# Keys and values of a latent attention as pairs of half-height products on TensorE

## The chip, the cores and the metric

The kernel runs on one core of one Trainium2 chip, in float32. The metric is the device time of one execution in microseconds. TensorE multiplies; ScalarE, VectorE and GpSimd read and write the on-chip memory (SBUF), the first two also the accumulators (PSUM, eight banks of 128 partitions by 512 float32 columns); SyncE issues nearly all the transfers (DMAs), in one queue. Each engine executes its own instructions in the order in which they were written and waits on semaphores for the others.

## The reference, cut to what matters

The input is x of 8 batches, 512 tokens and 256 features. Four residual blocks follow each other: attention A, a feed-forward block (256 to 1024 to 256, relu), attention B (scores times a decay mask, no softmax), and the feed-forward block again with the same weights. Each is applied to a layer norm of x and added to x. The change lies in attention A, which has 16 heads of 16 features:

```python
q  = x @ Wq + bq
kv = (x @ Wkv_down + bkv_down) @ Wkv_up + bkv_up       # 256 -> 64 -> 512
k, v = jnp.split(kv.reshape(B, T, 16, 32), 2, axis=-1)
q, k = apply_rope(q), apply_rope(k)
att = softmax(q @ k.T / sqrt(16) + bias(distance))
out = att @ v
out = out + 0.2 * sigmoid(q @ mean_k) * mean_v
return out @ Wo + bo
```

The 64 features between Wkv_down and Wkv_up are the latent. Keys and values are products over these 64 features.

## The kernel before, in words

**Stages of one batch.** The front of attention A (`front1`, `front2`) makes from x the layer norm, its transpose `xT` (256 features in two chunks of 128 partitions, by 512 tokens), the latent `lat` (64 partitions by 512 tokens), then keys, queries and values, and the means for the last term. Scores and softmax run per group of four heads in steps. The rest (`rest`: output projection, feed-forward, attention B, feed-forward) runs in units on TensorE.

**Keys, queries, values.** `latent` (line 338) multiplies two chunks of `wd_sb` by `xT` into rows 0 to 63 of a bank, and ScalarE copies it out with the bias and a sum over tokens. `half_unit` (line 394) makes one rotary half (the first or second eight features of all 16 heads) of keys or queries: a product into one bank, for keys `wk_sb[:, e, :]` (64 rows by 128 columns) by the latent, and then two VectorE operations that multiply the biased result by the cosine and the sine table into `rc` and `rs` (names in the profile). `turn` adds and subtracts the halves on GpSimd, stores them to a DRAM buffer and loads them from there per head into `kT` or `qT`: two DMAs and four DMAs. `values` (line 347) makes the values of two of the four token tiles (128 tokens each): two products with a latent tile as the stationary operand into the two halves of one bank, then two VectorE additions of the bias row into `vaug`. It is called twice a batch.

**Operands' rows.** A product over 64 partitions uses the rows of TensorE at which its operands' partitions lie. All operands of the keys and values lie on partitions 0 to 63. The score products are over 32 partitions, one head each, at the four offsets 0, 32, 64 and 96; a step makes two score products for the row maxima (s in the profile), which go with two of the offsets, and two for the probabilities (t), which go with the other two.

**Banks.** Scores have two buffers of two banks, weighted values one bank, and everything else takes the next of a ring of three banks (`misc`, line 203). In the first 34 steps the t products take two banks of that ring as well. A bank is free for its next user when its readers have finished.

**The order of the work** is written out when the program is built. The front of batch 0 comes first, by hand: `order0[:8]` runs from the latent to the queries, then late loads, then `order0[8:12]`. From there a planner keeps a clock for each engine and a time at which each of the three banks comes free. Each `Unit` has a cost on TensorE in ns (`pe`), costs on other engines (`then`) and predecessors. Between steps the planner issues the unit that can start earliest, as a credit of TensorE time per step allows or when a unit fits in front of the next step (lines 745 to 790, and the loop at the end). So a changed cost can move other units.

The loads at the start stand in SyncE's queue in the order of the program (lines 108 to 129): x in two halves, `vec` (bias columns), `wd_sb`, `wk_in`, `wq_in`, the rotary tables, `wv_sb`, bias rows, and attention B's weights. `regroup` (line 209) sorts the columns of `wk_in` and `wq_in` by halves on ScalarE, ahead of the copies of the first `xT`.

Of the kernel before, what the change touches and what calls it, by code (L numbers as in the profile page):

```python
# [15 lines left out]
P = 128  # L16
B, T, D = 8, 512, 256
NH, HD = 16, 16
HH = 8
# [16 lines left out]
def tile_kernel(  # L36
# [74 lines left out]
    half = keep([P, NT], "half")  # L111
    gps.memset(half, -0.5)
    vec = resident(vecs, "vec")
    wd_sb = resident(wdown, "wd_sb")

    wk_in = at.tile([LAT, NH, 32], F32, tag="p", bufs=4, name="wk_in")
    move(wk_in.rearrange("p h d -> p (h d)"), wk[:, 0, :])
    wq_in = at.tile([P, NC, NH, 32], F32, tag="p", bufs=4, name="wq_in")
    move(wq_in.rearrange("p c h d -> p c (h d)"), wq[:, :, 0, :])

    rope_sb = keep([P, 2, T], "rope_sb")
    move(rope_sb, rope[0:HH].unsqueeze(0).to_broadcast([NH, HH, 2, T]))
    wv_sb = resident(wv, "wv_sb")
    row = keep([P, 2, D], "row")
    move(row[:, 0, :], rows[0:D].partition_broadcast(P))
    move(row[:, 1, :], rows[2 * D : 3 * D].partition_broadcast(P))
    wqk_in = rs.tile([P, NC, 2, D], F32, tag="big", bufs=1, name="wqk_in")
    move(wqk_in, wb[:, :, 0:2, :])
    bv, b2 = row[:, 0, :], row[:, 1, :]


    qT = [keep([P, NG, T], f"qT{i}") for i in range(2)]
# [72 lines left out]


    wq_sb = keep([P, NC, 2, P], "wq_sb")
    wk_sb = keep([LAT, 2, P], "wk_sb")
    def regroup():
        for e in range(2):  # L210
            half_of = slice(e * HH, (e + 1) * HH)
            act.copy(wk_sb[:, e, :].rearrange("p (h d) -> p h d", d=HH), wk_in[:, :, half_of])
        for e in range(2):
            half_of = slice(e * HH, (e + 1) * HH)
            for c in range(NC):
                act.copy(wq_sb[:, c, e, :].rearrange("p (h d) -> p h d", d=HH), wq_in[:, c, :, half_of])
# [64 lines left out]
    class Unit:  # L281
        def __init__(self, fn, pe=0, then=(), after=(), step=0, gives=None, needs=(), bank=True):
            self.fn, self.pe, self.then, self.after, self.step = fn, pe, then, list(after), step
            self.gives, self.needs, self.bank, self.done = gives, needs, bank and pe > 0, None
            self.takes = self.frees = False


# [49 lines left out]
    def front1(b):  # L337
        def latent():
            ps = misc(f"lat_{b}")
            for c in range(NC):  # L340
                mm(ps[:LAT, :], wd_sb[:, c, :], xT_a[b]["xT"][:, c, :], c == 0, c == NC - 1)
            lt = fr.tile([LAT, T], F32, tag="lat", name=f"lat_{b}")
            lsum[b] = fr.tile([LAT, 1], F32, tag="lsum", name=f"lsum_{b}")
            act.activation(lt, ps[:LAT, :], AF.Identity, bias=vec[:LAT, V_BD : V_BD + 1], accum_out=lsum[b])
            lat_a[b] = lt

        def values(h):
            ps = misc(f"v_{b}_{h}")
            for i in range(2):
                t = 2 * h + i  # L350
                mm(ps[:, i * D : (i + 1) * D], lat_a[b][:, t * P : (t + 1) * P], wv_sb)
            for i in range(2):
                dve.tensor_tensor(
                    vaug[b % 2][:, 2 * h + i, : NH * 17].rearrange("p (h d) -> p h d", d=17)[:, :, :HD],
                    ps[:, i * D : (i + 1) * D].rearrange("p (h d) -> p h d", d=HD),
                    bv.rearrange("p (h d) -> p h d", d=HD),
                    ALU.add,
                )


        def mean_v():
            ps = misc(f"mv_{b}")
            for c in range(NC):
                mm(ps[:, c : c + 1], wv_sb[:, c * P : (c + 1) * P], lsum[b])
            m = fr.tile([P, NC], F32, tag="mv_a", name=f"mv_a_{b}")
            dve.scalar_tensor_tensor(m, ps[:, :NC], 0.1 / T, bvc, ALU.mult, ALU.add)
            for c in range(NC):
                gps.tensor_scalar(vmean[:, c, : NH + 1], vmask[:, c, :], m[:, c : c + 1], None, ALU.mult)

        def through_wo():  # L370
            ps = misc(f"me_{b}")
            for c in range(NC):
                mm(ps[:, :D], vmean[:, c, :], wo_sb[:, c, :], c == 0, c == NC - 1)
            dve.tensor_add(mem[b % 2][: NH + 1, :], ps[: NH + 1, :D], bo_row[: NH + 1, :])

        s, (h0, h1) = ln_units(lambda: xs[b], f"a{b}", fr)
        free = PER * (b - 1) + LAG + PVLAG + 2
        u = {"lat": Unit(latent, 1720, (("ACT", 700),), after=[h0[2], h1[2]])}
        for h in range(2):
            u["v", h] = Unit(  # L380
                lambda h=h: values(h), 900, (("DVE", 850),), after=[u["lat"]], step=free
            )
        u["mv"] = Unit(mean_v, 250, (("DVE", 150), ("POOL", 400)), after=[u["lat"]])
        u["me"] = Unit(through_wo, 900, (("DVE", 400),), after=[u["mv"]], needs=(("wo", b - 2),))
        xT_a[b] = s
        return h0 + h1, u
# [3 lines left out]
    def front2(b, u1):  # L390
        rot = {}
        cos, nsin = rope_sb[:, 0, :], rope_sb[:, 1, :]

        def half_unit(j, e):
            ps = misc(f"{'qk'[j]}{e}_{b}")
            if j == 0:
                for c in range(NC):
                    mm(ps, wq_sb[:, c, e, :], xT_a[b]["xT"][:, c, :], c == 0, c == NC - 1)
            else:
                mm(ps, wk_sb[:, e, :], lat_a[b])  # L400
            for n, table in (("c", cos), ("s", nsin)):
                t = fr.tile([P, T], F32, tag="rot", bufs=6, name=f"r{n}{j}{e}_{b}")
                dve.scalar_tensor_tensor(t, ps, qk_bias[:, j, e : e + 1], table, ALU.add, ALU.mult)
                rot[n, e] = t

        def turn(j):

            d = (dq, dk)[j][b % 2]
            for e in range(2):
                o = rot["c", e]  # L410
                if e == 0:
                    gps.tensor_add(o, o, rot["s", 1])
                else:
                    gps.tensor_sub(o, o, rot["s", 0])
                move(d[:, e * HH : (e + 1) * HH, :], o)
            src = d.rearrange("(g s) r t -> s r g t", s=4)
            to = (qT, kT)[j][b % 2]
            for h in range(4):
                move(to[h * 32 : h * 32 + HD], src[h])
            if j == 0:  # L420
                if b > 1:
                    move(to[HD:P:32], zero_rows)
                rot["q"] = rot["c", 0], rot["c", 1]

        def mean_k():
            m = fr.tile([P, 2], F32, tag="mk", name=f"mk_{b}")
            for e in range(2):
                unused = fr.tile([P, T], F32, tag="unused", name=f"unused{e}_{b}")
                act.activation(unused, rot["c", e], AF.Identity, accum_out=m[:, e : e + 1])
                gps.tensor_scalar(kmean[:, e, :NH], hmask, m[:, e : e + 1], None, ALU.mult)  # L430

        def gate():
            ps = misc(f"ga_{b}")
            for e in range(2):
                mm(ps, kmean[:, e, :], rot["q"][e], e == 0, e == 1)
            act.activation(gates[b % 2][:NH, :], ps[:NH, :], AF.Tanh)

        free = PER * (b - 1) + LAG + PVLAG + 2
        lat = u1["lat"]
        rope = (("DVE", 1550),)  # L440
        k = [Unit(lambda e=e: half_unit(1, e), 950, rope, after=[lat]) for e in range(2)]
        kt = Unit(lambda: turn(1), then=(("POOL", 2600),), after=k, step=free)
        km = Unit(mean_k, then=(("ACT", 1200), ("POOL", 400)), after=[kt])
        q = [Unit(lambda e=e: half_unit(0, e), 1720, rope, after=[lat]) for e in range(2)]
        qt = Unit(lambda: turn(0), then=(("POOL", 2600),), after=q, gives=("qk", b))
        ga = Unit(gate, 1720, (("ACT", 600),), after=[km, qt], needs=(("wo", b - 2),))
        return [lat] + k + [kt, km] + q + [qt, u1["v", 0], u1["v", 1], ga, u1["mv"], u1["me"]]


    def score_item(n):  # L450
# [271 lines left out]
    n0[1].fn(), n1[1].fn()  # L722
    n0[2].fn(), n1[2].fn()
    memory_buffers()
    for u in order0[:8]:
        u.fn()
    late_loads()
    plain(0), plain(1)
    for u in order0[8:12]:
        u.fn()  # L730
    product(), product_biases()
    buffers(1, gps)
# [12 lines left out]
    def start_of(u):  # L745
        if any(x not in given for x in u.needs) or any(a.done is None for a in u.after):
            return None
        if u.takes and held:
            return None
        t = max([a.done for a in u.after] + [clock["PE"] if u.pe else 0])  # L750
        return max(t, banks[0]) if u.bank else t

    def fetch(b):
        xs[b] = load_x(b)
# [2 lines left out]
    def issue(u):  # L757
# [5 lines left out]
        for e, ns in u.then:  # L763
            clock[e] = t = max(clock[e], t) + ns + 60
        u.done = t
        if u.bank:
            banks.popleft()
            banks.append(t)
        if u.takes:
# [89 lines left out]

    posts = []  # L860
    setup = [Unit(lambda: fetch(2), step=20)]
    for u in front[0][0] + order0[:12]:
        u.done = 0
    order0[12].step = 10
    chains = [order0[12:], setup]
    for b in range(1, B):
        ln0, u1 = front1(b)
        ln0[0].step = ln0[3].step = max(0, PER * (b - 1) + 2)
# [165 lines left out]
```

## Time and profile before

| | |
|---|---|
| time of three runs, median (lowest to highest) | 1354.7 us (1354.05 to 1356.53) |
| the profiled execution's own time | 1355.33 us |
| its span, first to last instruction | 1353.5 us |
| TensorE products busy | 1278.4 us |
| VectorE busy | 805.8 us |
| ScalarE busy | 450.8 us |
| GpSimd busy | 408.3 us |
| mean granted TensorE clock | 0.977 |

PE is TensorE's products and PEld its weight loads, DVE is VectorE, ACT ScalarE, POOL GpSimd, SP SyncE. A group in the profile has the form output <- inputs, then rows and columns of TensorE, shapes and count; its columns are busy time, mean ns of one, and the idle time ahead of it with what ended most of it. Busy times of products overlap and their ends are modelled, so the start of the next operation is the better measure of what one costs. L198 is the helper that issues every product and L69 the one that issues the operations of the other engines, so the names of tiles tell the lines apart. A line of the list of waits has the total, the number of times and the longest, in us; a line of the timeline has start, length, what it is, and in brackets the idle time before it and what ended it.

### The profile page before, as it was taken

To read this page: it belongs to the slowest core of one execution; us is meant where nothing else is said; L and a number is where in the kernel's file an instruction comes from. 1 tells how busy PE (TensorE), PEld (TensorE's weight loads), DVE (VectorE), ACT (ScalarE), POOL (GpSimd) and SP (SyncE) were. 2 spreads that over 40 slices of the span, in tenths; PEclk is the share of its full clock that TensorE was granted. 3 is DMA by queue.
4 is the path that set the end of the run, shared out by engine and by line. 5 is a ranking of instruction groups with operands and counts; after the bars stand their busy time and mean duration, and the time that the engine had idled before them with its cause. 6 is when DMAs were issued, how large, how long until landed. Compare 5 with 4: busy or idle time off the path is not lost. (4 is left out here: it accounts for less than half of the span.)

```text
span 1353.5 us, 15551 instructions
## 1 busy us (share of the span) xinstructions
PE 1278.4 (94%) x6116; PEld 632.2 (47%) x6116; DVE 805.8 (60%) x1323; ACT 450.8 (33%) x646; POOL 408.3 (30%) x461
## 2 busy tenths in 40 slices
PE   7889998999899998999999999999999999999989
PEld 3323233535354553545544454535444554455665
DVE  4577976678656686546765667646755484433120
ACT  2034434342434324333343323342343233331201
POOL 4165443233422323223331414213321232222010
PEclk9689989999999999999999999999999999999999
DMA  4440040003000210004000300003000000000000
GB/s 122 134 79 1 1 79 1 1 16 64 1 1 1 63 33 1 0 5 91 1 1 1 68 28 1 1 1 79 1 1 0 17 1 1 1 16 1 0 16 16
DMA packets 22159, 32.09 MB, mean 24 GB/s; under 512 B 2987, under 2 KB 12652, under 8 KB 21806
## 3 DMA queue, kind: packets, MB, share of 16 engines
q1 hardware_dynamic: 21446, 30.83, 10.2%
q8 instruction: 48, 0.79, 0.3%
q10 hardware_dynamic: 640, 0.26, 0.1%
q14 instruction: 25, 0.20, 0.0%
HBM read 18.24 MB, written 12.58 MB: 23 GB/s over the span
## 5 line engine op out<-in xcount | busy, mean ns | idle before, releaser
L69 DVE TENSOR_REDUCE mr<-s 128x2 f32<-128x1024 f32 x256 | 312.4, 1221 | 274.9 <-PE t L198 264.5
L69 ACT ACTIVATE p<-t 128x1024 f32<-128x1024 f32 (+1 forms) x290 | 264.0, 924 | 554.4 <-PE t L198 496.1
L69 POOL TENSOR_TENSOR p<-p,dec_a 128x512 f32<-128x512 f32 x182 | 233.1, 1302 | 490.0 <-ACT p L69 435.6
L198 PE MATMUL s<-kT,qT 32*128 32x512 f32 x1024 | 297.6, 664 | 40.3 <-DVE mr L69 36.5
L198 PE MATMUL t<-qT,kT 32*128 32x512 f32 x1024 | 297.0, 647 | 4.8 <-DVE mr L69 2.5
L69 DVE TENSOR_TENSOR p<-p,dec_a 128x512 f32<-128x512 f32 x330 | 230.1, 738 | 21.5 <-ACT p L69 21.3
L198 PE MATMUL x<-w_sb,h_x 128*128 128x256 f32 x1024 | 233.1, 383 | 0.0
L198 PEld LDWEIGHTS x<-w_sb,h_x 128*128 128x128 f32 x1024 | 190.7, 190 | 52.5 <-issue 27.6
L198 PEld LDWEIGHTS s<-kT,qT 32*128 32x128 f32 x1024 | 81.1, 189 | 208.1 <-DVE mr L69 85.2
L198 PE MATMUL pv<-p,va 128*32 128x512 f32 x1024 | 152.2, 614 | 3.7 <-DVE p L69 3.1
L69 ACT ACTIVATE h_x<-hx,vec 128x512 f32<-128x512 f32 x128 | 88.0, 688 | 156.3 <-PE hx L198 156.3
L198 PE MATMUL hx<-xT_g,w_sb 128*128 128x512 f32 x256 | 122.1, 622 | 0.7 <-ACT xT_g L69 0.7
L198 PE MATMUL hx<-xT_f,w_sb 128*128 128x512 f32 x256 | 119.0, 604 | 0.0
L69 DVE TENSOR_TENSOR x<-x,x 128x256 f32<-128x256 f32 x64 | 27.1, 424 | 153.9 <-PE x L198 153.8
L198 PEld LDWEIGHTS t<-qT,kT 32*128 32x128 f32 x1024 | 80.4, 184 | 22.0 <-issue 9.1
L198 PEld LDWEIGHTS hx<-xT_g,w_sb 128*128 128x128 f32 x256 | 48.0, 196 | 67.7 <-issue 59.8
L198 PEld LDWEIGHTS hx<-xT_f,w_sb 128*128 128x128 f32 x256 | 46.2, 192 | 57.5 <-issue 54.3
L198 PEld LDWEIGHTS pv<-p,va 128*32 128x32 f32 x1024 | 23.6, 108 | 78.2 <-issue 35.4
L69 POOL TENSOR_TENSOR x<-x,row 128x256 f32<-128x256 f32 x64 | 47.7, 765 | 38.4 <-DVE xn_g L69 20.4
L69 POOL TENSOR_TENSOR rc<-rc,rs 128x512 f32<-128x512 f32 x32 | 42.6, 1354 | 10.9 <-DVE rs L69 10.9
L198 PE MATMUL bs<-xT_r,ret 128*128 128x512 f32 (+3 forms) x128 | 38.3, 442 | 0.4 <-DVE mv_a L69 0.4
L198 PE MATMUL bo<-ret 128*128 128x256 f32 x160 | 36.7, 382 | 0.0
(130 smaller groups left out, 1034.5 us busy)
## 6 DMA issues: line engine op xcount, KB each, us to landing
dk<-rc SPq DMA_DIRECT2D x16, 256.0 KB
kT<-dk SPq DMA_DIRECT2D x32, 128.0 KB
dq<-rc SPq DMA_DIRECT2D x16, 256.0 KB
qT<-dq SPq DMA_DIRECT2D x32, 128.0 KB
out_dram<-x SPq DMA_DIRECT2D x32, 128.0 KB
x<-in_x_dram SPq DMA_DIRECT2D x7, 512.0 KB
w_sb<-in_w_dram SPq DMA_DIRECT2D x2, 1024.0 KB
x<-in_x_dram SPq DMA_DIRECT2D x2, 256.0 KB
```

The source lines that it names most:

```text
L69: ins = f(*a, **k)
L198: tc.keep_in_program_order(nc.tensor.matmul(o, lhsT=l, rhs=r, start=start, stop=stop))
```

## The change

The latent is computed on both halves of the partitions: the down weights stand twice side by side in `wd_sb`, so that the same two products fill 128 rows of the bank, and the copy out and its sum run over 128 partitions. For this the down bias of `vec` is loaded also to partitions 64 to 127. `wv_sb` is loaded twice, to both halves of the partitions, and `wk_in` too; `wk_sb` has the first rotary half on partitions 0 to 63 and the second on 64 to 127.

The two products of the keys thereby use different halves of TensorE's rows and go into two banks, issued one after the other in one unit. Values of token tiles 0 and 2 use the lower half, of 1 and 3 the upper, with one bank for each half: four products in alternation, and then four additions. Keys and values are each one unit instead of two, with a cost on TensorE of 950 ns each instead of two of 950 and two of 900. Such a unit takes two of the ring's three banks, and the planner starts it when the second comes free. Four DMAs are added at the start.

```diff
-    wd_sb = resident(wdown, "wd_sb")
-
-    wk_in = at.tile([LAT, NH, 32], F32, tag="p", bufs=4, name="wk_in")
-    move(wk_in.rearrange("p h d -> p (h d)"), wk[:, 0, :])
+
+    wd_sb = keep([P, NC, 2, LAT], "wd_sb")
+    for j in range(2):
+        move(wd_sb[:, :, j, :], wdown)
+
+    wk_in = at.tile([P, NH, 32], F32, tag="p", bufs=4, name="wk_in")
+    for j in range(2):
+        move(wk_in[j * LAT : (j + 1) * LAT].rearrange("p h d -> p (h d)"), wk[:, 0, :])
...
-    wv_sb = resident(wv, "wv_sb")
+    wv_sb = keep([P, D], "wv_sb")
+    for j in range(2):
+        move(wv_sb[j * LAT : (j + 1) * LAT], wv)
...
     bv, b2 = row[:, 0, :], row[:, 1, :]
+    move(vec[LAT:, V_BD : V_BD + 1], vecs[:LAT, V_BD : V_BD + 1])
...
-    wk_sb = keep([LAT, 2, P], "wk_sb")
+    wk_sb = keep([P, P], "wk_sb")
     def regroup():
         for e in range(2):
             half_of = slice(e * HH, (e + 1) * HH)
-            act.copy(wk_sb[:, e, :].rearrange("p (h d) -> p h d", d=HH), wk_in[:, :, half_of])
+            act.copy(
+                wk_sb[e * LAT : (e + 1) * LAT, :].rearrange("p (h d) -> p h d", d=HH),
+                wk_in[e * LAT : (e + 1) * LAT, :, half_of],
+            )
...
-            self.gives, self.needs, self.bank, self.done = gives, needs, bank and pe > 0, None
+            self.gives, self.needs, self.banks, self.done = gives, needs, int(bank) if pe > 0 else 0, None
...
-                mm(ps[:LAT, :], wd_sb[:, c, :], xT_a[b]["xT"][:, c, :], c == 0, c == NC - 1)
-            lt = fr.tile([LAT, T], F32, tag="lat", name=f"lat_{b}")
-            lsum[b] = fr.tile([LAT, 1], F32, tag="lsum", name=f"lsum_{b}")
-            act.activation(lt, ps[:LAT, :], AF.Identity, bias=vec[:LAT, V_BD : V_BD + 1], accum_out=lsum[b])
+                mm(ps, wd_sb[:, c].rearrange("p j n -> p (j n)"), xT_a[b]["xT"][:, c, :], c == 0, c == NC - 1)
+            lt = fr.tile([P, T], F32, tag="lat", name=f"lat_{b}")
+            lsum[b] = fr.tile([P, 1], F32, tag="lsum", name=f"lsum_{b}")
+            act.activation(lt, ps, AF.Identity, bias=vec[:, V_BD : V_BD + 1], accum_out=lsum[b])
             lat_a[b] = lt
 
-        def values(h):
-            ps = misc(f"v_{b}_{h}")
+
+        def values():
+            ps = [misc(f"v_{b}_{j}") for j in range(2)]
             for i in range(2):
-                t = 2 * h + i
-                mm(ps[:, i * D : (i + 1) * D], lat_a[b][:, t * P : (t + 1) * P], wv_sb)
-            for i in range(2):
-                dve.tensor_tensor(
-                    vaug[b % 2][:, 2 * h + i, : NH * 17].rearrange("p (h d) -> p h d", d=17)[:, :, :HD],
...
+                for j in range(2):
+                    rows_of = slice(j * LAT, (j + 1) * LAT)
+                    t = 2 * i + j
+                    mm(ps[j][:, i * D : (i + 1) * D], lat_a[b][rows_of, t * P : (t + 1) * P], wv_sb[rows_of])
+            for j in range(2):
+                for i in range(2):
+                    dve.tensor_tensor(
+                        vaug[b % 2][:, 2 * i + j, : NH * 17].rearrange("p (h d) -> p h d", d=17)[:, :, :HD],
...
-        for h in range(2):
-            u["v", h] = Unit(
-                lambda h=h: values(h), 900, (("DVE", 850),), after=[u["lat"]], step=free
-            )
+        u["v"] = Unit(values, 950, (("DVE", 1650),), after=[u["lat"]], step=free, bank=2)
...
-        def half_unit(j, e):
+        def projected(j, e):
             ps = misc(f"{'qk'[j]}{e}_{b}")
...
-                mm(ps, wk_sb[:, e, :], lat_a[b])
+                rows_of = slice(e * LAT, (e + 1) * LAT)
+                mm(ps, wk_sb[rows_of], lat_a[b][rows_of])
+            return ps
+
+        def keys():
+            ps = [projected(1, e) for e in range(2)]
+            for e in range(2):
+                half_unit(1, e, ps[e])
+
+        def half_unit(j, e, ps):
...
-        k = [Unit(lambda e=e: half_unit(1, e), 950, rope, after=[lat]) for e in range(2)]
+        k = [Unit(keys, 950, rope + rope, after=[lat], bank=2)]
...
-        return max(t, banks[0]) if u.bank else t
+        return max(t, banks[u.banks - 1]) if u.banks else t
...
-        if u.bank:
+        for _ in range(u.banks):
             banks.popleft()
             banks.append(t)
```

The means of the values read the lower half of `wv_sb` and of the sums alone, and the counts of `order0` that are written out by hand follow the two units fewer (`[:7]`, `[7:10]`, `[10:]`).

More of the change, by code (lines that the diff above doesn't have):

```diff
@@ L340, in latent @@
             for c in range(NC):
-                mm(ps[:LAT, :], wd_sb[:, c, :], xT_a[b]["xT"][:, c, :], c == 0, c == NC - 1)
-            lt = fr.tile([LAT, T], F32, tag="lat", name=f"lat_{b}")
-            lsum[b] = fr.tile([LAT, 1], F32, tag="lsum", name=f"lsum_{b}")
-            act.activation(lt, ps[:LAT, :], AF.Identity, bias=vec[:LAT, V_BD : V_BD + 1], accum_out=lsum[b])
+                mm(ps, wd_sb[:, c].rearrange("p j n -> p (j n)"), xT_a[b]["xT"][:, c, :], c == 0, c == NC - 1)
+            lt = fr.tile([P, T], F32, tag="lat", name=f"lat_{b}")
+            lsum[b] = fr.tile([P, 1], F32, tag="lsum", name=f"lsum_{b}")
+            act.activation(lt, ps, AF.Identity, bias=vec[:, V_BD : V_BD + 1], accum_out=lsum[b])
             lat_a[b] = lt
-        def values(h):
-            ps = misc(f"v_{b}_{h}")
+        def values():
+            ps = [misc(f"v_{b}_{j}") for j in range(2)]
             for i in range(2):
-                t = 2 * h + i
-                mm(ps[:, i * D : (i + 1) * D], lat_a[b][:, t * P : (t + 1) * P], wv_sb)
-            for i in range(2):
-                dve.tensor_tensor(
-                    vaug[b % 2][:, 2 * h + i, : NH * 17].rearrange("p (h d) -> p h d", d=17)[:, :, :HD],
-                    ps[:, i * D : (i + 1) * D].rearrange("p (h d) -> p h d", d=HD),
-                    bv.rearrange("p (h d) -> p h d", d=HD),
-                    ALU.add,
-                )
+                for j in range(2):
[6 more added lines that the diff above has]
+                        vaug[b % 2][:, 2 * i + j, : NH * 17].rearrange("p (h d) -> p h d", d=17)[:, :, :HD],
+                        ps[j][:, i * D : (i + 1) * D].rearrange("p (h d) -> p h d", d=HD),
+                        bv.rearrange("p (h d) -> p h d", d=HD),
+                        ALU.add,
+                    )
         def mean_v():
@@ L363, in mean_v @@
             for c in range(NC):
-                mm(ps[:, c : c + 1], wv_sb[:, c * P : (c + 1) * P], lsum[b])
+                mm(ps[:, c : c + 1], wv_sb[:LAT, c * P : (c + 1) * P], lsum[b][:LAT])
             m = fr.tile([P, NC], F32, tag="mv_a", name=f"mv_a_{b}")
@@ L378, in front1 @@
         u = {"lat": Unit(latent, 1720, (("ACT", 700),), after=[h0[2], h1[2]])}
-        for h in range(2):
-            u["v", h] = Unit(
-                lambda h=h: values(h), 900, (("DVE", 850),), after=[u["lat"]], step=free
-            )
+        u["v"] = Unit(values, 950, (("DVE", 1650),), after=[u["lat"]], step=free, bank=2)
         u["mv"] = Unit(mean_v, 250, (("DVE", 150), ("POOL", 400)), after=[u["lat"]])
@@ L440, in front2 @@
         rope = (("DVE", 1550),)
-        k = [Unit(lambda e=e: half_unit(1, e), 950, rope, after=[lat]) for e in range(2)]
+        k = [Unit(keys, 950, rope + rope, after=[lat], bank=2)]
         kt = Unit(lambda: turn(1), then=(("POOL", 2600),), after=k, step=free)
         km = Unit(mean_k, then=(("ACT", 1200), ("POOL", 400)), after=[kt])
-        q = [Unit(lambda e=e: half_unit(0, e), 1720, rope, after=[lat]) for e in range(2)]
+        q = [Unit(lambda e=e: half_unit(0, e, projected(0, e)), 1720, rope, after=[lat]) for e in range(2)]
         qt = Unit(lambda: turn(0), then=(("POOL", 2600),), after=q, gives=("qk", b))
         ga = Unit(gate, 1720, (("ACT", 600),), after=[km, qt], needs=(("wo", b - 2),))
-        return [lat] + k + [kt, km] + q + [qt, u1["v", 0], u1["v", 1], ga, u1["mv"], u1["me"]]
+        return [lat] + k + [kt, km] + q + [qt, u1["v"], ga, u1["mv"], u1["me"]]
     def score_item(n):
@@ L724, in tile_kernel @@
     memory_buffers()
-    for u in order0[:8]:
+    for u in order0[:7]:
         u.fn()
@@ L728, in tile_kernel @@
     plain(0), plain(1)
-    for u in order0[8:12]:
+    for u in order0[7:10]:
         u.fn()
@@ L861, in tile_kernel @@
     setup = [Unit(lambda: fetch(2), step=20)]
-    for u in front[0][0] + order0[:12]:
+    for u in front[0][0] + order0[:10]:
         u.done = 0
-    order0[12].step = 10
-    chains = [order0[12:], setup]
+    order0[10].step = 10
+    chains = [order0[10:], setup]
     for b in range(1, B):
```

## The prediction

> **What bounds the kernel now.** I read first the page's busy table and its 40 slices:
>
> ```profile
> PE 1278.4 (94%) x6116; PEld 632.2 (47%) x6116; DVE 805.8 (60%) x1323; ACT 450.8 (33%) x646; POOL 408.3 (30%) x461
> PE   7889998999899998999999999999999999999989
> DVE  4577976678656686546765667646755484433120
> ```
>
> TensorE (PE) is the bound from about 290 us on: between 290 and 1200 us the table of windows gives it 880.45 of 910 us. Before that VectorE is close behind: 88.77 of 118.7 us between 39.3 and 158 us, with TensorE at a mean clock of 0.86. A microsecond taken from TensorE is worth a microsecond only where TensorE does not wait next. So the second view is the groups, with the changed operations (count, busy us, mean ns):
>
> ```profile
> L198 PE MATMUL k<-lat,wk_sb 64*128 64x512 f32 x32 | 17.6, 675 | 0.9 <-ACT lat L69 0.9
> L198 PE MATMUL lat<-xT_a,wd_sb 128*64 128x512 f32 x32 | 17.2, 663 | 1.4 <-ACT xT_a L69 1.4
> L198 PE MATMUL v<-wv_sb,lat 64*128 64x256 f32 x64 | 16.5, 392 | 0.2 <-ACT wr L69 0.2
> ```
>
> A float32 product is two passes, so 32 rows of k are two products in each of 8 batches. The third view is the list of waits. One entry matters, TensorE waiting for the row maxima that free a score bank:
>
> ```profile
> PE s L198 <- DVE mr L69: 36.5, 41, 1.9
> ```
>
> The fourth is the timeline, for what a pair costs. First a lone pair of 32-row score products (start, length), then the keys of batch 3:
>
> ```profile
> 280.95 1.13 PE L198 MATMUL t<-qT,kT 32*128 32x512 f32 x4 [0.15 <-DVE mr L69]
> 282.01 0.66 PE L201 MATMUL tr_a<-ident,xn_a 128*128 128x128 f32 x4
> ...
> 288.06 1.98 PE L198 MATMUL k<-lat,wk_sb 64*128 64x512 f32 x4
> 289.97 1.98 PE L198 MATMUL b<-xT_r,ct 128*128 128x512 f32 x4
> ```
>
> Four passes in two row groups take 282.01 - 280.95 = 1.06 us from start to next start; the same four passes of the keys, all on rows 0 to 63, take 1.91. And what follows the keys of batch 4:
>
> ```profile
> 422.35 1.98 PE L198 MATMUL k<-lat,wk_sb 64*128 64x512 f32 x4
> ...
> 424.80 0.74 DVE L69 SCALAR_TENSOR_TENSOR rc<-k,qk_bias,rope_sb 128x512 f32<-128x512 f32 x1
> ...
> 426.78 0.74 DVE L69 SCALAR_TENSOR_TENSOR rs<-k,qk_bias,rope_sb 128x512 f32<-128x512 f32 x1
> 426.78 1.13 PE L198 MATMUL s<-kT,qT 32*128 32x512 f32 x4 [0.17 <-ACT p L69]
> 427.44 1.21 DVE L69 TENSOR_REDUCE mr<-s 128x2 f32<-128x1024 f32 x1
> ...
> 428.70 1.13 PE L198 MATMUL t<-qT,kT 32*128 32x512 f32 x4 [0.79 <-DVE mr L69]
> ```
>
> The keys have ended at 424.26, but VectorE, full since 422.46, runs four rope operations to 427.44 and only then the maximum for which TensorE waits.
>
> **What the Trainium skill says.** TensorEngine Tiling (Array Packing), Available Configurations, lists 2x row tiling of 64x128 with two independent tiles. The trace shows the overlap for 32 rows (1.06 us above); nothing in it shows two 64-row tiles together. The same page's Gotcha 1 says that row tiles must not write one PSUM bank at a time; the change takes two banks. TensorE: Matmul & The Clock Gate, The mechanism, says weight loads overlap running products only where the row group differs, and LDWEIGHTS prices a load by columns, P/1.2 ns: the trace agrees, 146 ns mean for lat's 64 columns against 190 to 202 for 128.
>
> **The change, part by part.**
>
> *Keys.* Two products one after the other become a pair: 1.91 to 1.06, -0.85 us a batch. If 64-row tiles do not run together: 0. More than halving (-0.95) is excluded.
>
> *Values.* Eight passes of 256 columns take 1.92 us (308.73 to 310.65), a pass starting each 0.216 us in the run at 27.9 us. Now four rounds of two. A lone pair's round costs 0.53 for a pass that takes 0.43, so 0.10 us of weight load lies open. If that is open once: 4 x 0.22 + 0.10 = 0.97 us; if in each round: 4 x (0.22 + 0.10) = 1.28. No row shows successive rounds on one row group, so I take 1.1: -0.8, between -0.65 and -0.95 (0 without overlap).
>
> *Latent.* The same four passes, 64 columns more per load: 0.05 us, one load open, +0.05; up to 0.2 if all four are. ScalarE's copy costs the same on twice the partitions (682 ns is by its 512 columns; 128-partition copies of that length take 688).
>
> Sum: -0.85 - 0.8 + 0.05 = -1.6 us of TensorE time a batch, 7 x 1.6 = 11.2 us in the seven batches whose front is planned among other work.
>
> *VectorE* has the same operations, and ends them no earlier: after a pair, four ropes run from 1.06 to 1.06 + 4 x 0.66 = 3.7 us; before, the second half was ready at 1.91 and ended at about 1.91 + 1.4 = 3.3 to 3.8. Where TensorE next waits for VectorE the gain is swallowed. Going by the timeline with the order as it is:
> - keys of batches 2, 4, 6, 7: waits of 1.72, 0.17+0.79, 0.23+0.78, 0.17+0.80 us on ScalarE or the maxima follow within 8 us: 0. Batch 1: VectorE-bound, then 0.60 for a probability tile: 0. Batch 3: a 0.53 wait follows at 301.95: 0.3 left. Batch 5: 12 passes of hidden layer follow: 0.85.
> - values of batch 1: 2.31 us for a bank held by `va`: 0; batch 6: 1.40 on a maximum: 0; batch 2: 0.4, a step soon waits; batches 3, 4, 5, 7: 0.8 each.
>
> That is 0.3 + 0.85 + 0.4 + 3.2 = 4.75 us. But the order is not kept: the planner counts 950 ns where it counted 1900 (keys) and 1800 (values), sees VectorE's 3.1 us after the keys, and fills a gap ahead of a step with any unit that fits. Of the other 11.2 - 4.75 = 6.4 us I give it a little over a quarter: 6.5 us in all.
>
> *Banks.* Keys and values now take two of the ring's three banks at once. In all seven loop batches the keys already ran back to back, in five the values too, so the holding is much as before; I cost it at nothing, covered by the third bank. Without cover it is a wait like the 2.31 us.
>
> *Loads.* Four DMAs more on SyncE's queue: second wdown, wk, wv and 64 words of vec, by the issue rows 0.43 + 0.57 + 0.60 + 0.46 = 2.1 us. Two stand ahead of wq_in: 1.0 us, and 192 KB more at some 250 GB/s is 0.8. wq_in's copies began on ScalarE at 8.16, and the first latent-input copy queues behind them (9.02 to 9.61); the one that matters starts at 11.68 after transposes. 2.07 us of slack hides 1.0. The vec words are read at 16.03 and would be issued at about 8.5; the like-sized bvc took from 10.45 to 13.22. Hidden, unless it takes over 7 us. The gate, bo_row and bvc loads move back 2 us; GpSimd idles 8.70 us after them.
>
> *Start.* At the half clock a pair takes 2.0 us (the first 28 score passes, seven pairs, took 53.29 - 39.31 = 13.98). Keys start at 16.86, ropes at 19.0 as now, and end at 21.7 instead of 22.1; queries start 1.6 us earlier, but their DRAM stores stand behind the four kT loads on SyncE (27.68 to 29.43). First scores, now at 39.31, come 0.4 to 0.9 earlier: -0.5.
>
> Total -7.0 us. The profiled execution took 1355.33 us (span 1353.5, 1.8 around it), 0.6 above the median of 1354.7; 1355.33 - 7.0 = 1348.3 there, 1347.7 on the median's scale.
>
> **Rivals.**
> - *All of it is recovered* (the planner fills each gap): -11.2 - 0.5 = 1343.0. For: TensorE is busy 97% from 290 us. Against: the 36.5 us of waits on maxima, which the planner did not fill before.
> - *The gain becomes waiting for VectorE*: a shuffled order meets as many new waits as it saves, about 1354. For: five of seven keys are followed by such a wait.
> - *No overlap on 64 rows* (the change does not do what it says): +0.05 a batch, start unchanged: about 1355. Against: 32-row pairs overlap to 1.06 us.
> - *Slower: the two-bank hold.* A unit of keys or values holds two banks until VectorE's last operation, and TensorE's next units stand with one. Price: the 2.31 us at 93.04 is this wait once. Fourteen units have 11.7 us to lose: past 0.84 us a unit it eats the gain, past 1.03 it is measurably slower; at 1.2 us, 1354.7 + 16.8 - 11.7 = 1360. Against: that wait was seen once in 14 places, with nearly the same holding.
>
> **How the numbers follow.** Partial gain (1345.5 to 1351) 0.46, full 0.23, swallowed 0.13, no overlap 0.07, bank hold 0.11. 0.2% is 2.7 us, about what a measurement can tell from no change. Faster 0.46 + 0.23 = 0.69; same 0.13 + 0.07 = 0.20; slower 0.11. Leaving out part of the bank hold above and the tail of the full gain below, the range is 1340 to 1358; the order's own scatter of a few microseconds is in it.
>
> **What would show it.** The k group at about 1.06 us from its start to the next operation's and v at 1.0 to 1.3 show the pairs; TensorE's busy sum should fall by about 12 us. If it falls and the span does not, the wait for maxima will have grown from 36.5 us; rows of TensorE waiting for `rc`, `rs` or `va` mean the bank hold. A first score later than 39.3 us means that a load was not hidden. The prediction is wrong if pairs run in series, or if the new order moves the idle 75 us (1353.5 - 1278.4) by more than 5.

## The result: 12.9 us less, and the profile after

The changed kernel took 1342.24 us in the median of four runs (1340.85 to 1343.83), the kernel before 1355.15 in four (1354.05 to 1356.53). The ratio is 0.9905, with a 95% interval of 0.9887 to 0.9922. The profiled execution took 1341.52 us with a span of 1339.7, against 1355.33 and 1353.5. In the changed kernel L205 is the helper that issues the products, L208 the one for transposes.

The page's busy table after:

```profile
PE 1256.3 (94%) x6116; PEld 623.3 (47%) x6116; DVE 811.0 (61%) x1323; ACT 450.0 (34%) x646; POOL 405.8 (30%) x461
```

TensorE is busy 22.1 us less, but idle 83.4 us (1339.7 - 1256.3) instead of 75.1 (1353.5 - 1278.4). Its changed groups after (busy us, mean ns, then the idle time ahead):

```profile
L205 PE MATMUL lat<-xT_a,wd_sb 128*128 128x512 f32 x32 | 17.5, 673 | 1.6 <-ACT xT_a L69 1.6
L205 PE MATMUL k<-lat,wk_sb 64*128 64x512 f32 x32 | 11.6, 703 | 0.9 <-ACT lat L69 0.9
L205 PE MATMUL v<-wv_sb,lat 64*128 64x256 f32 x64 | 9.8, 404 | 1.4 <-ACT wr L69 1.3
```

One product of a pair takes no less than before (703 ns against 675); two now run in the same time. Keys and values together lost 17.6 - 11.6 + 16.5 - 9.8 = 12.7 us of the 22.1. The wait for maxima in the list of waits after:

```profile
PE s L205 <- DVE mr L69: 44.4, 43, 2.4
```

It grew from 36.5 us. The timeline of TensorE after, at the keys of batch 4 (start, length):

```profile
421.48 1.13 PE L205 MATMUL k<-lat,wk_sb 64*128 64x512 f32 x4
422.54 3.72 PE L205 MATMUL x<-w_sb,h_x 128*128 128x256 f32 x16
426.19 0.70 PE L205 MATMUL s<-kT,qT 32*128 32x512 f32 x2
426.20 0.70 PE L205 MATMUL t<-qT,kT 32*128 32x512 f32 x2
```

The keys cost 422.54 - 421.48 = 1.06 us. What follows is new: sixteen products of the feed-forward block stand ahead of the next step, and that step's s and t start together. In the kernel before, s of the second step after these keys started at 426.78 and t, alone, at 428.70.

The clearest difference of place lies in batch 1. Milestones by the start of the n-th score step: step 17 at 84.39 us before and 83.00 after (1.4 apart), step 25 at 112.55 and 106.09 (6.5 apart). So 5.1 us come from 24 us of the run, with the same products in between in both. Later milestones move by up to 9 us either way from one group of eight steps to the next, since other units stand ahead of them. TensorE's timeline there, before:

```profile
87.67 1.99 PE L198 MATMUL v<-wv_sb,lat 64*128 64x256 f32 x8
...
93.04 1.85 PE L198 MATMUL t<-qT,kT 32*128 32x512 f32 x2 [2.31 <-DVE va L69]
94.82 3.78 PE L198 MATMUL ga<-rc,kmean 128*128 128x512 f32 x4
98.53 1.01 PE L198 MATMUL mv<-lsum,wv_sb 64*128 64x1 f32 x4
```

And after:

```profile
86.28 1.92 PE L205 MATMUL v<-wv_sb,lat 64*128 64x256 f32 x8
88.67 1.12 PE L205 MATMUL ga<-rc,kmean 128*128 128x512 f32 x2 [0.46 <-POOL rc L69]
90.34 1.13 PE L205 MATMUL ga<-rc,kmean 128*128 128x512 f32 x2 [0.55 <-POOL rc L69]
91.65 0.57 PE L205 MATMUL mv<-lsum,wv_sb 64*128 64x1 f32 x4 [0.18 <-DVE va L69]
92.15 0.70 PE L205 MATMUL s<-kT,qT 32*128 32x512 f32 x2
```

The planner now puts the gate's products (`ga`) and those of the value means (`mv`) ahead of the score step. Before, the step came first and its second probability product stood 2.31 us for a bank. The table of windows shows what that wait brought with it (length, then busy us and count of PE, PEld, DVE, ACT, POOL; then the granted clock, DMA share, GB/s). Before:

```profile
90.00:95.00 5.00, 2.69 (x9) 0.49 (x4) 4.68 (x7) 0.67 (x2) 3.36 (x3) 0.82 0.40 105
95.00:100.00 5.00, 5.00 (x12) 2.12 (x16) 0.16 (x1) 1.11 (x2) 1.43 (x2) 0.50 0.91 126
100.00:105.00 5.00, 5.00 (x25) 1.77 (x20) 1.54 (x2) 1.44 (x3) 0.49 (x2) 0.65 0.30 84
```

After:

```profile
90.00:95.00 5.00, 4.48 (x22) 2.27 (x26) 3.85 (x8) 1.67 (x3) 1.87 (x4) 1.00 0.51 136
95.00:100.00 5.00, 4.74 (x36) 1.59 (x28) 3.35 (x5) 2.56 (x5) 2.23 (x3) 1.00 1.07 165
```

Before, TensorE ran at half clock from 93.2 to 103.5 us, busy for all of the time between 95 and 100 us; after, the clock there is 1.00. The counts of passes, 12 and 36, do not compare directly, since those after are mostly score passes that run several at a time; the same four passes of `ga` took 3.71 us from start to next start before, and after twice 1.12 us for two. Whether this belongs to the pairs or to the order is the question of the experiments.

### The profile page after: what moved, and what is told of

Read it like the earlier page. It is cut to its first block, busy times and chain, and to the rows that moved or that the text cites. A ratio compares the mean times of both kernels' runs of the same rounds, so it can differ in the third digit from the quotient of the medians.

```text
span 1339.7 us, 15533 instructions
## 1 busy us (share of the span) xinstructions
PE 1256.3 (94%) x6116; PEld 623.3 (47%) x6116; DVE 811.0 (61%) x1323; ACT 450.0 (34%) x646; POOL 405.8 (30%) x461
## 5 line engine op out<-in xcount | busy, mean ns | idle before, releaser
L205 PE MATMUL s<-kT,qT 32*128 32x512 f32 x1024 | 295.3, 660 | 49.3 <-DVE mr L69 44.4
L205 PE MATMUL t<-qT,kT 32*128 32x512 f32 x1024 | 294.7, 642 | 0.3 <-ACT p L69 0.3
L205 PE MATMUL x<-w_sb,h_x 128*128 128x256 f32 x1024 | 233.9, 384 | 0.0
L205 PEld LDWEIGHTS x<-w_sb,h_x 128*128 128x128 f32 x1024 | 190.8, 190 | 54.5 <-issue 30.1
L205 PEld LDWEIGHTS s<-kT,qT 32*128 32x128 f32 x1024 | 81.2, 189 | 221.8 <-DVE mr L69 97.5
L205 PE MATMUL pv<-p,va 128*32 128x512 f32 x1024 | 151.7, 612 | 2.9 <-DVE p L69 2.4
L205 PE MATMUL hx<-xT_f,w_sb 128*128 128x512 f32 x256 | 120.2, 609 | 0.7 <-ACT xT_f L69 0.7
L205 PE MATMUL hx<-xT_g,w_sb 128*128 128x512 f32 x256 | 119.3, 609 | 0.7 <-ACT xT_g L69 0.7
L205 PEld LDWEIGHTS t<-qT,kT 32*128 32x128 f32 x1024 | 80.5, 184 | 15.9 <-ACT p L69 7.8
L205 PEld LDWEIGHTS hx<-xT_g,w_sb 128*128 128x128 f32 x256 | 46.8, 193 | 63.5 <-issue 58.1
L205 PEld LDWEIGHTS hx<-xT_f,w_sb 128*128 128x128 f32 x256 | 46.5, 194 | 58.3 <-issue 51.6
L205 PEld LDWEIGHTS pv<-p,va 128*32 128x32 f32 x1024 | 23.3, 108 | 79.3 <-issue 37.0
L205 PE MATMUL bs<-xT_r,ret 128*128 128x512 f32 (+3 forms) x128 | 38.0, 442 | 0.0
L205 PE MATMUL bo<-ret 128*128 128x256 f32 x160 | 36.6, 383 | 0.0
```

The source lines that it names most:

```text
L205: tc.keep_in_program_order(nc.tensor.matmul(o, lhsT=l, rhs=r, start=start, stop=stop))
```

## Experiments

Two theories. **Overlap**: the time comes from the pairs, which take 0.85 us a batch each from keys and values. **Order**: it comes from where the planner, with other costs and other units, puts the units, and the pairs matter little. In each kernel below the whole computation is done. Ratios are to the kernel before, run on the same chip at the same time; they are taken over all executions and can differ a little from the ratios of the medians. Where I compare two experiments I divide their ratios and add the halves of their intervals in squares.

**The two apart: order by overlap.** In three kernels the sequence in which steps and units are issued is not planned but replayed from a list, recorded from the changed kernel or from the one before.

```diff
 # e1: the changed kernel's order; keys and values all on rows 0 to 63
-                rows_of = slice(e * LAT, (e + 1) * LAT)
+                rows_of = slice(0, LAT)       # the same for the values' rows
 # e2: the order before, unit for unit; pairs issued in the place of their first unit
 # e3: the order before, no pairs: only the four loads and the doubled latent
```

> The changed kernel with its order of work, banks, loads and doubled latent, but all products of keys and values on rows 0 to 63, so that nothing overlaps. Theory overlap (the gain is the 0.86 us that each of 5 pairs of keys and 6 of values saves after batch 0, and the 1.3 us at the start): 1342.2 + 9.4 + 1.3, 1352 to 1354, with the 5 us between the 17th and the 25th score step kept, then only if the rest costs more. Theory order (the new order alone is better): 1342 to 1346. Theory both (5 us from the order in batch 1, the rest from overlap): 1348 to 1351. In this trace k and v each take 1.9 us from start to next start.

> The order of work of the kernel before, unit for unit, with keys and values in pairs in the place of their first unit. The prediction's account of a kept order: 4.75 us in the loop and, as measured now, 1.3 at the start, so 1355.2 - 6 = 1349. If no gain is swallowed: 1355.2 - 11.2 - 1.3 = 1342.7. Theory clock (5 us of the gain is the half clock after the wait for va in batch 1, which this order keeps): the first 17 steps 1.3 us earlier, nothing more gained up to the 25th, 1347 to 1350 in all.

> The kernel before with the four more loads and the doubled latent alone: its order, products of keys and values on rows 0 to 63 one after the other. The prediction: all of it hidden but 0.05 us a batch, 1355 to 1356, first score product at 39 to 39.5 us. If the loads delay the start, 1356 to 1358.

| median us, ratio to before | no overlap | pairs |
|---|---|---|
| order before | e3: 1356.49, 1.0008 [0.9996, 1.002] | e2: 1351.72, 0.9975 [0.9966, 0.9983] |
| new order | e1: 1344.43, 0.9926 [0.9911, 0.9941] | the change: 1342.24, 0.9905 [0.9887, 0.9922] |

Down a column is the order: without any overlap it is worth 0.9926 / 1.0008, 0.82% or 11.1 us (± 2.6); with pairs 0.70%, 9.5 us (± 2.6). Along a row is the overlap: 0.33%, 4.5 us (± 2.0), in the order before, and 2.9 us (± 3.1) in the new one, not told from nothing. The order theory holds for most of the gain. What is called order here includes the banks: in the new order the two products of a unit have two banks at once, and the values alternate between them. The loads and the doubled latent are not told from nothing in e3; its interval allows up to 2.7 us.

In e1 the pairs are gone, as its groups show:

```profile
L205 PE MATMUL k<-lat,wk_sb 64*128 64x512 f32 x32 | 17.6, 675 | 0.9 <-ACT lat L69 0.9
L205 PE MATMUL v<-wv_sb,lat 64*128 64x256 f32 x64 | 16.2, 391 | 0.3 <-ACT wr L69 0.2
```

From e1 to the change, TensorE's time from start to next start falls by 6.0 us on keys and 5.9 on values, but the span only by 4.6 (1344.3 to 1339.7), and the medians by 2.2. By the same measure, waits behind them included, products on weighted values (+4.0), attention B's `b` (+2.6) and the transposed maxima (+0.9) take part of it back; this compares two single executions, and other groups differ by up to 1.8 us either way. At the keys of batch 4 nothing is left in these two executions of what batches 0 to 3 saved: they start at 421.48 us in both. In e2, too, waits take a part back; at the keys of batch 4:

```profile
422.15 1.13 PE L205 MATMUL k<-lat,wk_sb 64*128 64x512 f32 x4
...
426.05 1.13 PE L205 MATMUL s<-kT,qT 32*128 32x512 f32 x4 [0.17 <-ACT p L69]
428.50 1.43 PE L205 MATMUL t<-qT,kT 32*128 32x512 f32 x4 [1.32 <-DVE mr L69]
```

The keys are 0.85 us shorter than in the kernel before, and the wait for the maximum is 1.32 us instead of 0.79.

**Batch 1's gate alone.** Only two units move, in the replayed list of before:

```diff
 # e4 on e3 (no pairs), e8 on e2 (pairs); batch 1
-    v, v, STEP, ..., ga, ..., mv
+    v, v, ga, mv, STEP, ...
```

> The run without pairs in the old order, with one thing moved: in batch 1 the gate and the value means are issued before the score step that follows the values, as the changed kernel has it, instead of after it. Theory clock: TensorE no longer stands 2.3 us waiting for va in one piece, its clock stays at 1.0 between 90 and 105 us, and the run is 4 to 6 us shorter than the run with the old order and no pairs: 1350. If the order there is worth nothing: within 1 us of it.

> The old order with pairs, and the gate of batch 1 moved ahead of a score step as in the run without pairs. Theory clock (TensorE's half-clock time there is 10.2 us, worth 5): 2 to 5 us under the old order with pairs, 1347 to 1350, with no half clock between 85 and 105 us. If the gate's place is worth nothing once pairs are made: 1351 to 1352.

e4: 1354.16 us, 0.9977 [0.996, 0.9994], so 0.31% or 4.2 us (± 2.8) below e3. Its twelve times fall into two groups, four from 1346.47 to 1348.6 and eight from 1352.27 to 1355.15, so that the medians differ by 2.3 us only, and 1350 was expected; what parts the groups is open. e8: 1345.02 us, 0.9922 [0.9902, 0.9942], so 0.53% or 7.2 us (± 3.0) below e2. The windows of e2:

```profile
95.00:100.00 5.00, 5.00 (x7) 1.18 (x5) 1.15 (x2) 0.60 (x1) 1.26 (x1) 0.50 0.69 123
100.00:105.00 5.00, 5.00 (x22) 1.82 (x22) 0.24 (x2) 0.59 (x1) 0.66 (x2) 0.51 0.62 115
```

and of e8:

```profile
95.00:100.00 5.00, 5.00 (x35) 1.96 (x36) 3.81 (x5) 3.06 (x6) 2.50 (x2) 1.00 0.85 118
100.00:105.00 5.00, 5.00 (x34) 1.92 (x34) 4.20 (x7) 2.79 (x6) 2.78 (x3) 1.00 0.39 95
```

e2 has half clock from 94.7 to 104.9 us, e8 has none there. The price fits: 10.2 us at half the rate are 5.1, and e2's wait of 2.38 us at 94.50 becomes two of 0.46 and 0.55. It also fits over all executions: the mean granted clock is 0.975 in e2 and 0.980 in e8, worth up to some 6.5 us. So this one place of two units carries about 4.2 of the order's 11.1 us without pairs, and 7.2 of its 9.5 with them, each to within 3 us. The pairs are not needed for it: e1 and e4 have full clock there too.

**Which part of the planner's input makes the order.** The change lowers the costs and also merges two units into one with two banks.

```diff
 # e5, e6: the changed kernel with other costs on TensorE
-    Unit(keys, 950, ...),  Unit(values, 950, ...)
+    Unit(keys, 1060, ...), Unit(values, 1060, ...)       # e5: as measured
+    Unit(keys, 1900, ...), Unit(values, 1800, ...)       # e6: the old sum
 # e7: pairs, but planned as two units of one bank; the first issues the pair
-    Unit(key_unit(e), 950, ...), Unit(value_unit(h), 900, ...)
+    Unit(key_unit(e), 475, ...), Unit(value_unit(h), 475, ...)
```

> The changed kernel with 1060 ns as the planner's cost of a unit of keys and of values, which is what the trace shows, instead of 950. If the new order's gain of about 10 us belongs to what the units are (one unit, cheap, two banks): 1340 to 1345. If it is where a shuffle of units happened to land, so that another small shuffle lands elsewhere: anywhere from 1340 to 1352, and the time at half clock and the number of t products issued apart from s say where.

> The changed kernel, pairs and two-bank units as they are, but with the planner's costs of before in sum: 1900 ns for the keys and 1800 for the values. If the lower cost makes the good order: 1350 to 1353, as the old order with pairs (1351.7). If the merged unit or the two banks make it: 1341 to 1345.

> Pairs, planned as two units of one bank each as before, at 475 ns each (the first makes the pair, the second nothing). If the lower cost makes the good order: 1341 to 1345. If the merged unit or the two banks make it: 1350 to 1353.

e5: 1346.71 us, 0.9942 [0.9924, 0.9959]. e6: 1353.16, 0.9976 [0.9958, 0.9994]. e7: 1339.34, 0.9881 [0.9859, 0.9903]. With the units merged but priced as before (e6, twelve times from 1343.41 to 1356.42) the order's gain is lost: e6 is where e2 is. With the price halved but nothing merged (e7) all of it is kept; e7 is not told from the change (3.3 us ± 3.8). In these runs the gain goes with the price and not with the merging. What the price does is seen at the steps: a t product issued apart from s makes a step of 2.98 us (426.78 to 429.76 in the kernel before) where joint ones take 1.07. The traces have four such steps in the kernel before and in e2, e3, e4 and e8, two in e6, and none in the change, e1, e5 and e7. By the planner's rule a cheaper unit leaves credit, with which another unit can go ahead of the next step, as the sixteen products did above; the planner's own steps were not traced.

Batch 1's gate goes with the merging instead: e6 has it early, while e7 has it late and runs at half clock from 90.1 to 100.4 us. That e7 is the faster all the same (12.9 us ± 3.9) shows that the clock is not all of it: its mean granted clock, 0.975, is that of e2, and it takes 12.8 us (± 3.2) less. The same pairs in six orders (e2, e5, e6, e7, e8 and the change) spread from 1339.3 to 1353.2 us. A price nearer the measured 1.06 us (e5) was worse than 950 ns (5.1 us ± 3.4), in its traced execution with half clock at 963 and 1069 us and a longer stretch at the start that the changed kernel's doesn't have. So a truer price did not make a better order here.

**Keys and values apart**, in the new order:

> The new order with pairs of keys alone; values on rows 0 to 63. Between the run with no pairs (1344.4) and the changed kernel (1342.2). The trace of the changed kernel has real pairs of keys in batches 0 and 3 to 7. If the gain that is kept is the start's (queries begin 1.6 us earlier): first score product at 38 to 38.5 us, 1342 to 1343. If keys are swallowed by VectorE's rope operations, as the prediction has it: 1343.5 to 1344.5.

> The new order with pairs of values alone; keys on rows 0 to 63. Values pair in batches 0 and 2 to 7. The prediction keeps most of the values' gain: 1341 to 1343 by that account. If both halves are swallowed alike: 1343.5 to 1344.5. First score product at 39 to 39.7 us either way, since the queries wait for the keys.

Pairs for the keys alone (e9): 1346.67 us, 0.9933 [0.9917, 0.995]. For the values alone (e10): 1343.74, 0.9919 [0.9902, 0.9936]. Against e1 without pairs (0.9926) both are within the intervals, e9 on the slower side, against what was expected of it. In this order neither gain can be told from nothing.

**The half clock at the start.** The changed kernel runs at half clock from 33.8 to 61.1 us. It sets in 0.4 us after TensorE begins to wait for the first queries, a wait of 4.64 us that ends at 38.00. I filled that wait with products that nothing reads:

```diff
-    product(), product_biases()
+    product(); warm(3); product_biases(); warm(2)   # warm(n): n products of 128 x 512
```

> The changed kernel with five products of 128 rows by 512 columns, read by nobody, in the time in which TensorE waits for the first queries: three ahead of attention B's bias products and two after them. Theory clock: the 27 us at half clock from 34 us on begin because that stretch looks idle to the clock; with it filled the first seven score pairs take 1.1 to 1.3 us each instead of 2.0, and the run is 3 to 8 us shorter, 1334 to 1339. If score pairs, which use half of the rows, can't hold the clock up: within 1.5 us of 1342.2. If the five products themselves delay the first scores: 1343 to 1346.

> The same five products in the fastest run so far, the one planned as two units of half the cost (1339.3). Theory clock: 1331 to 1336. If the clock is not held: 1338 to 1341.

e11 (on the change) took 1342.54 us, 0.9909 [0.9889, 0.9929]: nothing. Its first score products:

```profile
39.28 3.61 PE L205 MATMUL s<-kT,qT 32*128 32x512 f32 x12
43.83 7.57 PE L205 MATMUL s<-kT,qT 32*128 32x512 f32 x16 [0.94 <-DVE mr L69]
```

against those of the change:

```profile
38.00 13.91 PE L205 MATMUL s<-kT,qT 32*128 32x512 f32 x28 [4.64 <-DMA qT<-dq]
```

The first twelve passes are fast, the next sixteen are at half clock again (43.7 to 60.8 us), and the first one starts 1.3 us later. e12 (the same on e7) took 1337.6 us, 0.9872 [0.9855, 0.989]. It is the fastest kernel measured, faster than both the kernel before and the change, but not told from e7 (0.9881).

## Why the prediction was right and wrong

- **Keys, -0.85 us: right.** 1.06 us from start to next start in batches 3 to 7, so the rival without overlap falls.
- **Values, -0.8: right.** 1.06 us in batches 2 to 7, at the short side of the 0.97 to 1.28 expected.
- **Latent, +0.05: right within what is seen.** From start to next start it sums to 17.64 us over 8 batches against 17.56. What is said there of weight loads, "the trace agrees", holds for the step and not for the size: P/1.2 ns (the Trainium skill, TensorE: Matmul & The Clock Gate, LDWEIGHTS) is 53 ns for 64 columns and 107 for 128, where the trace has 146 and 190 to 202. The difference, 44 to 56 ns, is what the +0.05 rests on.
- **Order as it is, 4.75 us, with 0.5 at the start: near in size.** The order before with pairs (e2) lies 4.5 us (± 2.0) below the same order without (e3). Below the kernel before itself it lies 3.4 (± 1.2), and it took 1351.7 us where this account let 1349 be expected. Its terms, batch by batch, were not tested.
- **Start, -0.5: there, but the loads can take it back.** From the first latent product to the first score, the eight kernels with all pairs take 25.2 to 26.3 us, the four without (before, e1, e3, e4) 27.0 to 27.5. But the first latent product itself moves, so that the first score starts at 38.0 us in the change, 38.9 in e5, 39.7 in e8 and 40.9 in e2, against 39.3 before.
- **Loads, "2.07 us of slack hides 1.0": wrong in part.** `wq_in` is issued 1.57 us later (4.88 against 3.31), not 1.0. In the thirteen traces with the added loads its copies on ScalarE begin at 9.7 to 12.8 us, against 8.16 before, and in five of them (e2, e5, e6, e8, e11) the first latent product starts 0.5 to 2.4 us later than the 12.32 of before. In the change it starts at 11.88. On the whole run this is not told from nothing: e3 carries all four loads at 1.0008 [0.9996, 1.002].
- **Banks at nothing: right in the sum, wrong in three places.** The third bank was not always there: in batches 1 and 2 the second keys product waited for its own. At batch 2's keys in the change (weight loads, idle in brackets):

```profile
156.50 0.29 PEld L205 LDWEIGHTS k<-lat,wk_sb 64*128 64x128 f32 x2 [0.76 <-issue]
157.36 0.30 PEld L205 LDWEIGHTS k<-lat,wk_sb 64*128 64x128 f32 x2 [0.56 <-ACT p L69]
```

  The second load starts 0.86 us after the first, and the keys take 1.90 us: no pair. In batch 1 they take 1.85, and there the values do not pair either (1.92). The cost is the lost overlap, not a longer wait; in the rival that ends slower it would have had to reach 0.84 us a unit in all fourteen.
- **Swallowed gains: right.** The wait for maxima grew to 44.4 us, and from e1 to the change 11.9 us of TensorE time on keys and values give 4.6 us of span in the profiled executions and 2.9 (± 3.1) over all.
- **The step that failed: "Of the other 11.2 - 4.75 = 6.4 us I give it [the re-planned order] a little over a quarter".** That took the planner's share to be a part of what the overlap saves. It is not bounded by that. The new order without any overlap (e1) is 11.1 us faster than the order before (e3). The forecast of -7.0 us against -12.9 measured is short mainly by this term: 1.75 us given, 9.5 to 11.1 measured. Along the table the 12.9 us are 1.1 more for loads and latent, 11.1 less for the order and 2.9 less for the pairs. That the measured time lies inside the stated 1340 to 1358 us is in good part luck: the range was drawn from what becomes of the overlap, with a few microseconds for the order's scatter, and the part expected most, 1345.5 to 1351, was missed.
- **Within it, "values of batch 1: 2.31 us for a bank held by `va`: 0".** I took the wait as a constant of the place. It was a matter of which unit stood ahead, and 10.2 us at half clock hung on it, which the kernel before showed in the windows at 90 to 105 us and which I did not price. e8 against e2: 7.2 us.
- **A sign of being wrong that the prediction named came true**: the new order was not to move the idle 75 us by more than 5, and moved them by 8.3, to 83.4.
- **TensorE busy, -12: -22.1 measured.** 12.7 of it are the pairs. From e3 to e1, with no pairs in either, half clock falls from 75.1 to 54.6 us in the profiled executions, worth up to 10.2, and the four lone steps take 7.0 us more than joint ones would. The sum, 17.2, is more than the span's 12.7 (1357.0 to 1344.3), so the two do not simply add. Over all executions the mean granted clock rises from 0.975 to 0.980, worth up to some 7.7 us. How the order's gain divides is thus not shown; only the gate of batch 1 was tested by itself.
- **The rival "all of it is recovered", 1343.0**, came within a microsecond of the time and is wrong in its cause: the planner did not turn the pairs' gain into time, it made another order that is faster without them.

What stays open: which single input (a step's credit, a bank's due time) moves each unit was not traced in the planner, and what makes e7's order fast at a low clock was not looked for.

## What to carry to other kernels

When a change alters costs or units that a planner reads, predict the re-planned order as a change of its own and not as a share of the saving: replay the old order with the new work and the new order with the old work, and the two part cleanly. Ahead of that, look in the windows of the kernel before for granted clock below 1 while TensorE is busy, and price each such stretch at half its length together with the wait that begins it, as something that another order can remove, or move elsewhere. Where several orders of the same work spread over 14 us, a gain of 2 us per batch or less should be judged in a fixed order.

## What the hardware showed that was not expected

A single wait of about 2.3 us can cost more in clock than in itself. In batch 1, before the step's second probability product, this is seen in all five kernels that have the wait: in the kernel before (2.31 us, ending at 93.04), e2 (2.38, at 94.50), e3 (2.30, at 95.75), e7 (2.38, at 89.98) and e12 (2.38, at 91.02) half clock began 0.1 to 0.2 us after its end and lasted 10.2 us, though TensorE was busy for all of it from 95 to 100 us in the kernel before. In the change and e8 waits of 0.46, 0.55 and 0.18 us with work between them were followed by none.

The length of a wait does not decide it alone. In the change and in e9, which has the same order, the same wait stands late in the run:

```profile
1062.98 0.70 PE L205 MATMUL s<-kT,qT 32*128 32x512 f32 x2 [2.30 <-DVE mr L69]
1065.84 0.76 PE L205 MATMUL s<-kT,qT 32*128 32x512 f32 x2 [2.30 <-DVE mr L69]
```

The first line is of the change, whose clock stays at 1.00 there; the second is of e9, where half clock begins at 1066.35 and lasts 3.4 us. A wait of 2.74 us in e7 (ending at 204.24) was followed by no half clock either. So a stretch that one trace shows at such a place need not be in every execution. The stretches are multiples of 3.41 us: 3.4, 6.8, 10.2, and 27.3 at the start. The Trainium skill, TensorE: Matmul & The Clock Gate, What's actually happening, describes a free-running window of 4096 cycles, 3413 ns, from whose activity the rate is set, and the lengths seen here agree with it. That it depends on where a wait falls in such a window would fit, but was not tested.

Score products on 32 rows ran on at half clock where they started so: between 40 and 50 us the change has TensorE busy 9.96 of 10 us at a clock of 0.50, and in e11 they fell back from full clock after 4.4 us (39.3 to 43.7). That it is their use of only part of the rows was not tested; the fall in e11 also lies in a wait of 0.94 us, which ends at 43.83.
